# Attention and octonion FFN on one core: stacked operand rows in another order, and masked maxima by one vector instruction per head

## The chip, the cores and the metric

The kernel runs on one NeuronCore of a Trainium2 chip. The metric is the device time of one launch in microseconds; 1092.06 us is the median of three runs before the change. In the text PE is TensorE (matmuls), DVE is VectorE, ACT is ScalarE, POOL is GpSimd, and SP is the engine whose queue issues most of the DMAs.

## What is computed

The input x has 2 sequences of 1024 tokens with 512 features, all in float32. Cut to what matters:

```python
xn = layernorm(x)

# attention: 32 heads of 16 dimensions
q, k, v = split(xn @ w_qkv.T + b_qkv)
scores = q @ k.T / sqrt(16) + alibi[head, key]      # 1024 x 1024 per head
scores = where(query >= key, scores, -1e9)          # causal
attn = softmax(scores)
s = (attn @ v) @ w_out.T + b_out

# FFN with ternary weights in octonion products, hidden width 1360
gate, up = oct_linear(xn, w_gate), oct_linear(xn, w_up)
g = silu(oct_linear(silu(gate) * up, w_down))

return x + s * g
```

The softmax subtracts each query's maximum over its allowed keys. The change is in how these maxima are formed and in how the operands of the score products reach SBUF.

## The kernel before

**Stages.** A lead-in normalises the first tokens and projects the first heads; attention runs from some 37 us to some 800 us; the FFN follows and ends the span.

**Attention.** Heads go in groups of four (g, 8 per sequence), queries in halves of 512 (qc). One *unit* is (sequence, group, half), 32 in all. For each unit the kernel does two passes over the scores. The first forms each query's maximum: queries on the 128 partitions, keys along the columns (line 553, into one of three PSUM banks x0, x1, x2). For the first half of the queries only the diagonal part exists; for the second half every query also sees the 512 keys of the left half, which need no mask (`left`, line 567, one reduction per head). The diagonal part (`diagonal`, line 569) goes by blocks of 128 queries, tl = 0 to 3, with (tl + 1) x 128 keys each; one bank holds four heads of 128 keys, two of 256, one of 384 or one of 512. There VectorE first adds a triangular mask to the last 128 columns of each head, in place in PSUM, and then reduces the whole bank to one maximum per head (`mx`).

`split_max` joins `mx` and `left` and splits the maxima into two float32r parts (`rm`), `place_max` (line 612) turns them on TensorE and ScalarE copies them to SBUF (`mr`), and POOL issues two DMAs that put them into the two last rows of the stacked queries. The second pass (line 669) multiplies with those rows, so that the scores come out with the maximum already subtracted, now with keys on the partitions; ScalarE takes the exponential (`p`), and line 707 multiplies with the values.

**Stacked operands.** To keep float32 accuracy with float32r products, q and k are split into a high and a low part. A stack (`q_stack`, `k_stack`, rings of 4 and 5) has 128 rows: 64 rows hold four pairings of 16 dimensions (k: high, low, high, low; q: high, high, low, low), then come rows for the alibi term and the maxima. The contraction runs over the rows. `qk_items` projects q and k for two groups at a time (16 matmuls of 512 columns), splits them into `st` (ScalarE and VectorE), and SP writes `st` to `sp` in DRAM. `fill_k` and `fill_q` (lines 514 and 527) read them back, one DMA for each of the four pairings: 16 partitions, four heads, 512 elements each, 128 KB. `fill_k` also loads two alibi rows. One stack half needs four such transfers; attention has 64 stack halves, so 256 transfers.

**Weights.** `load_wq` (line 143) loads the q and k weights of the next two groups into `wqr` with two DMAs of 512 KB on SP's queue, and `compact_wq` (line 151) has POOL copy them into `wq`. The load is emitted with the last product of the groups before.

**Order.** All instructions are emitted by a planner that runs on the host when the kernel is built (from line 1092). It keeps model times of TensorE, VectorE and ScalarE, of the PSUM banks and of the fills, and emits next what it thinks is ready first: maxima (`next_max`), exponentials (`next_exp`), products with values, projections and others. Each engine then executes in that order; a wait that the planner did not foresee holds up all that follows on that engine. Its prices of a fill are in `try_fill` (line 1135), those of the maxima in `next_max` (line 1159). SP's queue carries weights, staged writes, fills, the writes of attention's output and the output's loads, in order. The trace shows that SP has eight semaphores in turn for its transfers, so that a transfer is issued when the eighth before it has landed.

The mask is a [128, 512] tile of which only columns 384 to 511, the triangle, are loaded (line 1030); later, in the FFN, the same tile serves as a buffer.

Of the kernel before, what the change touches and what calls it, by code (L numbers as in the profile page):

```python
# [10 lines left out]
F32 = mybir.dt.float32  # L11
F32R = mybir.dt.float32r
AF = mybir.ActivationFunctionType
ALU = mybir.AluOpType
AX = mybir.AxisListType
# [3 lines left out]
P = 128  # L19
B, S, D = 2, 1024, 512  # L20
NT = B * S
H, HD = 32, 16
NG = H // 4
KD = D // P
# [51 lines left out]
def kernel(  # L76
# [31 lines left out]
    NP = NG // 2  # L108
# [34 lines left out]
    def load_wq(gp, eng):  # L143
        t = wqp.tile([P, 2, KD, 2, 4, 32], F32, tag="wqr", name=f"wqr_{gp[0]}_{gp[1]}")
        for n in range(2):
            eng.dma_start(
                out=t[:, n].rearrange("p k w h e -> p (k w h e)"), in_=wqk[2 * gp[1] + n]
            )
        wq_raw[gp] = t
# [256 lines left out]

    def q_of(b, g, half):
        return q_ring[(2 * (b * NG + g) + half) % 4]  # L410

# [49 lines left out]
    def qk_items(b, gp):  # L461

        box = {}

        def product(which, c, kt):
            if (which, c, kt) == (0, 0, 0):
                if (b, gp) not in wq_tiles:
                    compact_wq((b, gp))
                parts[b, gp] = [
                    spill.tile([2, P, S], F32, tag=f"sp{w}", name=f"sp_{b}_{gp}_{w}")  # L470
                    for w in range(2)
                ]
            if kt == 0:
                box["ps"] = ps_m.tile([P, 512], F32, tag="m", name=f"pqk_{b}_{gp}_{which}_{c}")
            ps = box["ps"]
            pe(
                nc.tensor.matmul(  # L477
                    ps,
                    lhsT=wq_tiles[b, gp][:, kt, which, :],
                    rhs=xnT[:, kt, b * S + c * 512 : b * S + (c + 1) * 512],  # L480
                    start=(kt == 0),
                    stop=(kt == KD - 1),
                )
            )
            n = b * NP + gp + 1
            if (which, c, kt) == (1, 1, KD - 1) and n < B * NP:
                load_wq((n // NP, n % NP), sp_)
            if kt < KD - 1:
                return
            bias = bqk_sb[:, 1 + 2 * (which * NP + gp) :][:, 0:1]  # L490
            st = stg.tile([P, 2, 512], F32R, tag="st", name=f"st_{b}_{gp}_{which}_{c}")
            act_.activation(st[:, 0, :], ps, AF.Identity, bias=bias)
            dve_.scalar_tensor_tensor(
                st[:, 1, :], ps, bias, st[:, 0, :].bitcast(F32), ALU.add, ALU.subtract
            )
            sp_.dma_start(
                out=parts[b, gp][which][:, :, c * 512 : (c + 1) * 512].rearrange(
                    "l p n -> p l n"
                ),
                in_=st.bitcast(F32),  # L500
            )

        return [
            (858, lambda w=w, c=c, kt=kt: product(w, c, kt), "qk" if kt == KD - 1 else None)
            for w in range(2)
            for c in range(2)
            for kt in range(KD)
        ]
# [5 lines left out]
    def fill_k(b, g, half):  # L514

        k = k_of(b, g, half)
        for r in range(4):
            sp_.dma_start(
                out=k[r * HD : (r + 1) * HD].bitcast(F32),
                in_=heads(parts[b, g // 2][1], r % 2, g, half * 512, 512),  # L520
            )
        sp_.dma_start(
            out=k[64:66].bitcast(F32),
            in_=al_dram[:, 4 * g : 4 * g + 4, half * 512 : half * 512 + 512],
        )

    def fill_q(b, g, half):

        q = q_of(b, g, half)
        for r in range(4):  # L530
            sp_.dma_start(
                out=q[r * HD : (r + 1) * HD].bitcast(F32),
                in_=heads(parts[b, g // 2][0], r // 2, g, half * 512, 512),
            )

# [2 lines left out]
    def max_items(b, g, qc):  # L538

        tiles = {}  # L540

        def begin():
            for name in ("left", "mx")[1 - qc :]:
                tiles[name] = wk.tile([P, 4, 4], F32, tag=name, name=f"{name}_{b}_{g}_{qc}")

        def products(tl, first, count, c, n):
            x_banks[0] += 1
            ps = ps_x.tile(
                [P, 512], F32, tag=f"x{x_banks[0] % 3}", name=f"s1_{b}_{g}_{4 * qc + tl}_{c}_{first}"
            )  # L550
            for j in range(count):
                pe(
                    nc.tensor.matmul(  # L553
                        ps[:, j * n : (j + 1) * n],
                        lhsT=q_of(b, g, qc)[0 : NR - 2, first + j, tl * P : (tl + 1) * P],
                        rhs=k_of(b, g, c)[0 : NR - 2, first + j, :n],
                        start=True,
                        stop=True,
                    )
                )  # L560
            return ps[:, 0 : count * n].rearrange("p (h n) -> p h n", n=n)

        def left(tl, i):
            if (tl, i) == (0, 0):
                begin()
            ps = products(tl, i, 1, 0, 512)
            dve_.tensor_reduce(tiles["left"][:, tl, i : i + 1], ps, AX.X, ALU.max)

        def diagonal(tl, first, count):
            if (qc, tl, first) == (0, 0, 0):  # L570
                begin()
            n = (tl + 1) * P
            ps = products(tl, first, count, qc, n)
            block = ps[:, :, tl * P : n]
            dve_.tensor_tensor(
                block,
                block,
                mask[:, 384:512].rearrange("p (h n) -> p h n", h=1).to_broadcast([P, count, P]),
                ALU.add,
            )  # L580
            dve_.tensor_reduce(
                tiles["mx"][:, tl, first : first + count], ps, AX.X, ALU.max
            )

        items = []
        for tl in range(4):
            if qc:
                for i in range(4):
                    items.append((1, 512, False, lambda tl=tl, i=i: left(tl, i)))
            count = (4, 2, 1, 1)[tl]  # L590
            for i in range(0, 4, count):
                items.append(
                    (
                        count,
                        (tl + 1) * P,
                        True,
                        lambda tl=tl, i=i, count=count: diagonal(tl, i, count),
                    )
                )
        return items, tiles  # L600
# [251 lines left out]
    for b in range(B):  # L852
        for hh in range(2):
            n = 2 * b + hh
# [172 lines left out]
        busy(2)  # L1027
    compact_wq((0, 0))
    load_wv(0)
    sp_.dma_start(out=mask[:, 384:512], in_=cmask[:, 384:512])  # L1030
    sp_.dma_start(out=bv_sb, in_=bv.partition_broadcast(P))
    stat(4)
# [102 lines left out]
    def try_fill():  # L1135

        n, part = divmod(fills[0], 4)
        if n >= B * NG or len(qk_done) <= (n // 2 + 1 if n > 1 else part // 2):
            return
        if n == 0 and now[0] < qk_done[part // 2] - 4000:  # L1140
            return
        if unit_of(exps, E[0]) < 2 * (n - 2) + (0, 1, 2, 2)[part]:
            return
        (fill_q if part % 2 else fill_k)(n // NG, n % NG, part // 2)
        fills[0] += 1
        link[0] = max(now[0], link[0], qk_done[n // 2 + 1 if n > 1 else part // 2]) + (4500 if n else 3000)
        fill_at.append(link[0] + 2500)

    def try_fetch():
        for n, k in enumerate(fetches):  # L1150
# [8 lines left out]
    def next_max(pos):  # L1159
        if M[0] == len(maxs):  # L1160
            return []
        u, n, count, heads_in, cost, diagonal, emit = maxs[M[0]]
        fill = 4 * (u // 2) + 1 + 2 * units[u][2]
        if fills[0] <= fill or n == 0 and u >= 2 and u - 2 not in placed:
            return []

        def go():
            emit()
            M[0] += 1
            run_pe("R", ready, heads_in * max(cost * 0.417 + 18, 108))  # L1170
            end = run_dve(
                now[0] + START,
                heads_in * cost * 1.04 + 70 + (heads_in * 135 + 70) * diagonal,
            )
            take(x_free)[0] = end + END
            if n == count - 1:
                split_max(*units[u], mtiles[u])
                turns.append((u, run_dve(end, 500) + END))

        mpos = at[u] + (at[u + 1] - at[u]) * n / count  # L1180
        lead = size[1] + size[0] * 0.6
        ready = max(fill_at[fill], min(x_free))
        return [(ready, 4 if mpos < pos + lead else 5.5, 0, go)]
# [433 lines left out]
```

## Time and profile before

| | us |
|---|---|
| runs, without profile | 1090.71, 1092.06, 1093.07 |
| profiled execution, its own time | 1090.84 |
| its span (first to last instruction) | 1089.0 |
| PE, DVE, ACT, POOL busy | 1036.4, 678.9, 508.3, 173.8 |
| DMA moved | 104.04 MB, mean 96 GB/s |

By stage, from the windows view (busy us of each engine; the clock is the granted TensorE clock as a share of full speed):

| window, us | PE | DVE | ACT | clock | DMA busy | GB/s |
|---|---|---|---|---|---|---|
| 0 to 40 | 35.5 | 21.6 | 13.3 | 1.00 | 0.78 | 223 |
| 40 to 80 | 31.7 | 29.9 | 8.0 | 0.91 | 0.94 | 156 |
| 80 to 160 | 73.3 | 68.5 | 36.4 | 0.90 | 0.61 | 138 |
| 160 to 240 | 73.9 | 60.2 | 52.9 | 0.97 | 0.35 | 81 |
| 240 to 320 | 75.7 | 59.0 | 47.8 | 0.98 | 0.62 | 126 |
| 320 to 400 | 79.6 | 63.7 | 43.7 | 1.00 | 0.48 | 97 |
| 400 to 480 | 78.7 | 60.9 | 40.8 | 1.00 | 0.45 | 102 |
| 480 to 560 | 79.4 | 68.2 | 45.9 | 1.00 | 0.47 | 99 |
| 560 to 640 | 79.8 | 62.4 | 40.6 | 1.00 | 0.43 | 78 |
| 640 to 760 | 118.5 | 91.3 | 72.4 | 1.00 | | |
| 760 to 820 | 54.0 | 26.5 | 39.8 | 0.97 | 0.27 | 82 |

How to read these: a busy share is time in which the engine had an instruction under way. Matmuls overlap, and their ends are modelled, so a TensorE that is busy all the time need not run at its peak. "DMA busy" is the mean over the 16 DMA engines of the share of time in which their packets are under way; packets of one engine can overlap, so over a few microseconds it can exceed 1. In the groups by line nearly all vector, scalar and DMA instructions carry line 69, a helper that records them, so they are told apart by the tiles that they write and read: `s` are scores in PSUM, `mx` and `left` the maxima.

### The profile page before, as it was taken

What the parts mean: (1) busy time and instruction counts of PE and PEld (TensorE: products, weight loads), DVE (VectorE), ACT (ScalarE), POOL (GpSimd) and SP (SyncE); (2) the same over time, 40 slices, a digit from 0 to 9 for tenths busy, and PEclk for the clock granted to TensorE, in tenths of its full rate; (3) what the DMA queues carried; (4) which work ended last, traced back from release to release, by engine and by line L of the source; (5) the groups of instructions that cost most, each with busy time, mean ns of one, the idle gap of its engine ahead of it and who ended that gap; (6) DMA issues with size and microseconds to landing.
All of it is one profiled execution on the core that took longest, in us unless ns stands there. A gap on an engine that the chain in (4) does not pass through costs nothing.

```text
span 1089.0 us, 15459 instructions
## 1 busy us (share of the span) xinstructions
PE 1036.4 (95%) x5578; PEld 696.3 (64%) x5578; DVE 678.9 (62%) x1406; ACT 508.3 (47%) x958; POOL 173.8 (16%) x288
## 2 busy tenths in 40 slices
PE   8798988998999999999999999999999999999995
PEld 5554656674666667556667566665456678888784
DVE  6668888774988867878878778858342123141312
ACT  4032647654665544555645455665581213232322
POOL 7501014001010011010011000010011123332322
PEclk9999979999999999999999999999999999999998
DMA  6986563525374454355354337741141113030211
GB/s 226 175 157 161 137 124 108 89 52 116 82 154 89 123 85 81 99 136 95 74 128 65 82 78 116 137 89 50 35 132 49 49 59 116 1 116 1 79 38 39
DMA packets 73195, 104.04 MB, mean 96 GB/s; under 512 B 25896, under 2 KB 30640, under 8 KB 73120
## 3 DMA queue, kind: packets, MB, share of 16 engines
q1 hardware_dynamic: 69648, 98.28, 40.2%
q0 software_dynamic: 3424, 4.64, 1.7%
q8 instruction: 45, 0.74, 0.3%
q14 instruction: 30, 0.25, 0.1%
q10 hardware_dynamic: 48, 0.13, 0.0%
HBM read 69.39 MB, written 33.10 MB: 94 GB/s over the span
## 4 chain that ended last, share of the span: by engine, by line
PE 76%; DVE 8%; issue 5%; DMA 5%; ACT 4%; POOL 2%; SPq 0%; DVEq 0%; POOLq 0%; ACTq 0%
PE po L707 12%; PE s L669 12%; PE s L553 11%; PE pqk L477 9%; PE pu L1436 6%; PE pg L1436 6%; PE pd L1478 6%; PE pout L776 5%; PE pv L435 4%; DVE mx L69 3%; PE s L688 2%; DMA q_stack<-mr 1%; ACT p L69 1%; PE pm L618 1%; DVE s L69 1%
## 5 line engine op out<-in xcount | busy, mean ns | idle before, releaser
L69 ACT ACTIVATE p<-s 128x512 f32<-128x512 f32 x576 | 317.5, 596 | 205.0 <-PE s L688 114.0
L669 PE MATMUL s<-q_stack,k_stack 128*128 128x512 f32 (+3 forms) x768 | 252.5, 397 | 10.3 <-ACT p L69 5.1
L553 PE MATMUL s<-k_stack,q_stack 126*128 126x512 f32 (+3 forms) x768 | 235.5, 391 | 15.3 <-DVE mx L69 7.7
L69 DVE TENSOR_REDUCE mx<-s 128x1 f32<-128x384 f32 (+3 forms) x352 | 226.2, 643 | 11.6
L69 DVE TENSOR_REDUCE left<-s 128x1 f32<-128x512 f32 x256 | 163.8, 684 | 49.7 <-PE s L553 49.3
L669 PEld LDWEIGHTS s<-q_stack,k_stack 128*128 128x128 f32 x768 | 133.1, 190 | 82.7 <-ACT p L69 37.3
L553 PEld LDWEIGHTS s<-k_stack,q_stack 126*128 126x128 f32 x768 | 131.3, 192 | 67.5 <-issue 23.0
L707 PE MATMUL po<-p,v 128*32 128x512 f32 (+3 forms) x1536 | 142.2, 492 | 0.4 <-ACT p L69 0.4
L69 DVE TENSOR_TENSOR s<-s,mask 128x128 f32<-128x128 f32 (+2 forms) x352 | 123.9, 352 | 29.0 <-PE s L553 28.1
L477 PE MATMUL pqk<-xnT,wq 128*128 128x512 f32 x256 | 132.3, 618 | 8.1 <-POOL wq L69 6.9
L69 DVE SCALAR_TENSOR_TENSOR h<-pu,sc_u,sg 128x512 f32<-128x512 f32 (+1 forms) x44 | 33.0, 751 | 156.6 <-PE pu L1436 155.6
L69 POOL DMA_DIRECT2D q_stack<-mr x64 | 32.2, 508 | 615.5 <-ACT mr L69 615.5
L69 POOL TENSOR_TENSOR hs<-h,hs 128x512 fp32r<-128x512 f32 (+1 forms) x43 | 56.3, 1310 | 215.5 <-ACT hs L69 215.5
L688 PE MATMUL s<-mask_r,ident_r 128*128 128x256 f32 (+1 forms) x320 | 89.0, 278 | 0.0
L707 PEld LDWEIGHTS po<-p,v 128*32 128x32 f32 x1536 | 42.3, 109 | 72.5 <-issue 65.3
L69 ACT ACTIVATE sg<-pg,sc_g 128x512 f32<-128x512 f32 (+1 forms) x44 | 30.2, 687 | 100.2 <-PE pg L1436 100.0
L435 PE MATMUL pv<-wv,xnT 128*128 128x256 f32 x256 | 68.3, 392 | 0.1
L477 PEld LDWEIGHTS pqk<-xnT,wq 128*128 128x128 f32 x256 | 46.4, 195 | 33.8 <-issue 20.3
L69 ACT CAST hs<-h 128x512 fp32r<-128x512 f32 (+1 forms) x44 | 27.2, 619 | 85.3 <-DVE h L69 85.3
L776 PE MATMUL pout<-wo_sb,oT 128*128 128x512 f32 x128 | 62.7, 604 | 0.5 <-ACT oT L69 0.5
L688 PEld LDWEIGHTS s<-mask_r,ident_r 128*128 128x128 f32 x320 | 60.5, 189 | 2.7 <-issue 1.7
L435 PEld LDWEIGHTS pv<-wv,xnT 128*128 128x128 f32 x256 | 47.0, 193 | 17.1 <-issue 8.4
(144 smaller groups left out, 1074.8 us busy)
## 6 DMA issues: line engine op xcount, KB each, us to landing
sp<-st SPq DMA_DIRECT2D x32, 512.0 KB
k_stack<-sp SPq DMA_DIRECT2D x128, 128.0 KB
q_stack<-sp SPq DMA_DIRECT2D x128, 128.0 KB
wqr<-in_wqk_dram SPq DMA_DIRECT2D x16, 512.0 KB
xt<-in_x_dram SPq DMA_DIRECT2D x16, 256.0 KB
att<-o SPq DMA_DIRECT2D x32, 128.0 KB
ot<-att SPq DMA_DIRECT2D x16, 256.0 KB
proj<-y SPq DMA_DIRECT2D x16, 256.0 KB
```

The source lines that it names most:

```text
L69: ins = issue(*args, **kwargs)
L435: nc.tensor.matmul(ps[:, 0:256], lhsT=xnT[:, c, b * S + kt * P : b * S + (kt + 1) * P], rhs=wv_tiles[2 * b + hh][:, c, :], start=(c == 0), ...
L477: nc.tensor.matmul(ps, lhsT=wq_tiles[b, gp][:, kt, which, :], rhs=xnT[:, kt, b * S + c * 512 : b * S + (c + 1) * 512], start=(kt == 0), st ...
L553: nc.tensor.matmul(ps[:, j * n : (j + 1) * n], lhsT=q_of(b, g, qc)[0 : NR - 2, first + j, tl * P : (tl + 1) * P], rhs=k_of(b, g, c)[0 : NR ...
L618: nc.tensor.transpose(ps[0:8, tl * P : (tl + 1) * P], tiles["rm"][:, tl].rearrange("p l h -> p (l h)"), ident,)
L669: nc.tensor.matmul(ps[:, c0 : c0 + w], lhsT=k_of(b, g, kt // 4)[0:NR, h, kt % 4 * P : (kt % 4 + 1) * P], rhs=q[0:NR, h, 512 - w : 512], st ...
L688: pe(nc.tensor.matmul(out, lhsT=ident_r, rhs=rhs, start=False, stop=True))
L707: nc.tensor.matmul(po[32 * i : 32 * i + 32, 512 - w : 512], lhsT=v[:, kt, h * VC : h * VC + 32], rhs=p[:, i * part + c0 : i * part + c0 + ...
L776: nc.tensor.matmul(ps, lhsT=turned[t][:, c, :], rhs=wo_sb[0][:, c, :], start=(c == 0), stop=(c == KD - 1),)
L1436: nc.tensor.matmul(ps[:fs, :], lhsT=fw[mt][:, n0 + kt, 0:fs], rhs=part[:, kt, :], start=(kt == 0 and n == 0), stop=(kt == KD - 1 and n == 1),)
L1478: nc.tensor.matmul(pd, lhsT=hs[k][:fs, n, st * P : (st + 1) * P], rhs=fw[mt][:fs, 8:12, :].rearrange("p s n -> p (s n)"), start=(mt == 0 a ...
```

## The change

Five things change.

1. `fill_k` and `fill_q`: pairing r goes to the partitions r, r + 4, ..., r + 60 instead of r x 16 to r x 16 + 15. q and k are permuted alike, so the products sum the same terms. Source, bytes and number of DMAs stay.
2. `diagonal`: for each head one `tensor_tensor_reduce` adds a mask over all (tl + 1) x 128 columns, in place, and writes the maximum of the sum into `mx`. Before, there were one add and one reduction per bank.
3. The mask's columns 0 to 383 are set to zero by POOL, before its triangle is loaded, so that a mask of any of the four widths can be taken from the tile's end.
4. `load_wq` is emitted after the last staged write of `qk_items` instead of before it, so it stands behind that write on SP's queue.
5. The planner's prices: a fill occupies the link for 2600 ns instead of 4500 (3000 for the first group) and is ready 2200 ns later instead of 2500; a diagonal bank costs VectorE 100 ns per head on top of 1.04 ns a column, instead of 140 ns and 135 ns per head.

```diff
@@ qk_items, product
-            n = b * NP + gp + 1
-            if (which, c, kt) == (1, 1, KD - 1) and n < B * NP:
-                load_wq((n // NP, n % NP), sp_)
             if kt < KD - 1:
                 return
...
                 in_=st.bitcast(F32),
             )
+            n = b * NP + gp + 1
+            if (which, c, kt) == (1, 1, KD - 1) and n < B * NP:
+                load_wq((n // NP, n % NP), sp_)
@@ fill_k
-                out=k[r * HD : (r + 1) * HD].bitcast(F32),
+                out=k[r:64:4].bitcast(F32),
@@ fill_q
-                out=q[r * HD : (r + 1) * HD].bitcast(F32),
+                out=q[r:64:4].bitcast(F32),
@@ max_items, diagonal
             ps = products(tl, first, count, qc, n)
-            block = ps[:, :, tl * P : n]
-            dve_.tensor_tensor(
-                block,
-                block,
-                mask[:, 384:512].rearrange("p (h n) -> p h n", h=1).to_broadcast([P, count, P]),
-                ALU.add,
-            )
-            dve_.tensor_reduce(
-                tiles["mx"][:, tl, first : first + count], ps, AX.X, ALU.max
-            )
+
+            for j in range(count):
+                dve_.tensor_tensor_reduce(
+                    out=ps[:, j, :],
+                    in0=ps[:, j, :],
+                    in1=mask[:, 512 - n : 512],
+                    scale=1.0,
+                    scalar=-3.0e38,
+                    op0=ALU.add,
+                    op1=ALU.max,
+                    accum_out=tiles["mx"][:, tl, first + j : first + j + 1],
+                )
@@ lead-in
     load_wv(0)
+    pool_.memset(mask[:, 0:384], 0.0)
     sp_.dma_start(out=mask[:, 384:512], in_=cmask[:, 384:512])
@@ try_fill
-        link[0] = max(now[0], link[0], qk_done[n // 2 + 1 if n > 1 else part // 2]) + (4500 if n else 3000)
-        fill_at.append(link[0] + 2500)
+        link[0] = max(now[0], link[0], qk_done[n // 2 + 1 if n > 1 else part // 2]) + 2600
+        fill_at.append(link[0] + 2200)
@@ next_max
-                heads_in * cost * 1.04 + 70 + (heads_in * 135 + 70) * diagonal,
+                heads_in * cost * 1.04 + (heads_in * 100 if diagonal else 70),
```

## The prediction

> **What bounds the kernel now.** I read the page's busy shares and its chain of waits first, then the chain in order of time, the DMA queue's own instructions, the windows, and last the vector engine's groups by form.
>
> ```profile
> PE 1036.4 (95%) x5578; PEld 696.3 (64%) x5578; DVE 678.9 (62%) x1406; ACT 508.3 (47%) x958; POOL 173.8 (16%) x288
> PE 76%; DVE 8%; issue 5%; DMA 5%; ACT 4%; POOL 2%; SPq 0%; DVEq 0%; POOLq 0%; ACTq 0%
> 33.79 8.37 DMA sp<-st
> 45.59 7.22 DMA q_stack<-sp
> 62.50 7.97 DMA q_stack<-mr
> 721.75 7.06 DMA q_stack<-mr
> ```
>
> TensorE bounds it: 95% busy, 76% of the chain. What the change can win lies in the other quarter. The last four lines are the largest transfers on the chain (start, us, what): three follow each other before the first exponential at 70.6 us, the fourth comes at the end of attention.
>
> ```profile
> 38.00:40.00 2.00, 2.00 (x13) 1.73 (x13) 1.81 (x4) 0.00 (x0) 1.60 (x31) 1.00 1.02 413
> 46.00:48.00 2.00, 1.84 (x8) 1.04 (x6) 1.93 (x5) 0.00 (x0) 0.00 (x0) 1.00 1.07 131
> 40.00:80.00 40.00, 31.73 (x126) 20.12 (x128) 29.93 (x59) 8.02 (x12) 4.57 (x39) 0.91 0.94 156
> 480.00:560.00 80.00, 79.36 (x498) 50.47 (x497) 68.21 (x144) 45.86 (x84) 6.02 (x9) 1.00 0.47 99
> ```
>
> The windows end with granted clock, DMA share and GB/s. From 38 to 40 us weights and staged projections (128 partitions each) move at 413 GB/s; from 46 to 48 us only fills run, each into 16 neighbouring partitions, and with the DMA engines just as full (1.07) they make 131 GB/s. Fills are the slow transfers, and there are 256 of 128 KB.
>
> ```profile
> 32.28 1.29 SPq L69 DMA_DIRECT2D wqr<-in_wqk_dram  x2
> 33.79 0.38 SPq L69 DMA_DIRECT2D sp<-st  x1
> 42.18 1.73 SPq L69 DMA_DIRECT2D k_stack<-sp  x4
> ...
> 86.71 1.29 SPq L69 DMA_DIRECT2D wqr<-in_wqk_dram  x2
> 92.61 0.38 SPq L69 DMA_DIRECT2D sp<-st  x1
> ```
>
> SP's queue: the weight load (2 x 512 KB) stands ahead of the last staged write, and the fill at 42.18 waits for that write to land.
>
> ```profile
> L69 DVE TENSOR_REDUCE mx<-s 128x1 f32<-128x512 f32 x128 | 88.5, 691 | 4.3
> L69 DVE TENSOR_TENSOR s<-s,mask 128x128 f32<-128x128 f32 x256 | 74.6, 291 | 18.3 <-PE s L553 17.6
> L69 DVE TENSOR_TENSOR s<-s,mask 128x256 f32<-128x256 f32 x64 | 27.2, 425 | 7.9 <-PE s L553 7.7
> L69 DVE TENSOR_TENSOR s<-s,mask 128x512 f32<-128x512 f32 x32 | 22.1, 692 | 2.8 <-PE s L553 2.8
> ```
>
> An add costs 0.15 us and 1.06 ns a column (291, 425 and 692 ns), a reduction of 512 as much as an add of 512.
>
> **The masked maxima.** Removed are 352 adds (74.6 + 27.2 + 22.1 = 123.9 us) and 352 reductions into mx (226.2 us in the page's group): 350 us, over 512 heads 0.68 us each. Added are 512 instructions, 128 of each width 128, 256, 384 and 512. The trace has none of this kind. Bounds: from below a plain add over the same columns, 0.291 + 0.425 + 0.558 (interpolated) + 0.692 = 1.97 us for four heads, 128 times = 252 us; from above the slowest two-input row, the tail's y<-ga_more,s_posb with 1501 ns for 512 columns, 2.93 ns a column, 128 x 1280 columns = 480 us. In between: an add and a separate read-out at 0.15 us (sc_g, one column) is 328 us. I take the add, because its row has the same operands (scores from PSUM, mask from SBUF): DVE loses 98 us of its 679.
>
> [...]
>
> What this is worth is read from the chain. By stage from 80 to 560 us it holds 28 us of DVE mx and 12 us of DVE s, 40 in all; a head of 512 stands there with 0.22 + 0.02 + 0.69 = 0.93 us. With 0.69 it is 26% shorter: 10.4 us. But TensorE works in those stretches too: from 362.9 to 367.0 us the matmuls that start fill 3.2 of 4.1 us at their own pitch (0.23 us for 512 columns), from 453.6 to 458.7 us 4.6 of 5.05. TensorE is late next there and lets through 22% and 9% of 40 us, 8.8 and 3.6. Between 560 and 640 us the chain holds no DVE at all, so there it is worth nothing. I take **8 us** (3.6 to 10.4).
>
> **Fills over 64 partitions.** Same bytes, same instructions, same operands in the product; only rows move. The bounds are 131 GB/s (no gain) and 413; the nearest row that writes 64 partitions is the load of w_g, which together with a staged write makes 243 GB/s at 0.97 from 22 to 24 us. I take 243: a group of four falls from 4.0 to some 2.2 us.
>
> [...]
>
> **The weight load behind the staged write.** At 33.79 us the write was ready earlier (its DVE instruction ends at 32.6), so the issue wins 1.1 us, and 1 MB at 413 GB/s (2.5 us) no longer stands ahead of it; faster fills ahead of it give 1 to 2 more: the landing at 42.16 comes some 5 us sooner. The load now lies between that write and the next fills, where SP's 3.4 us of issuing covers it. The fill that lands at 52.81 gains 3 more by the rate, and the row of maxima at 62.50 (8 KB, 7.97 us amid the fills, the tile's median is 2.3) some 4. That is 12 us on the chain, but the window 40 to 80 shows what TensorE can take back: 8.3 us idle and 9% of 40 us lost to the clock, 11.9. I take **9 us** (1 to 11.9).
>
> The same move costs once. At 86.71 us the load now stands behind the write at 92.61, which waits for DVE. TensorE stood 2.62 us until 93.20 for the weights that this load brings; POOL's compaction is queued behind the landing, and behind it on POOL the next rows of maxima. It would come 6 us later; a shorter DVE queue there (four heads and one block of 512, some 2 us) and other work in front of the product reduce it. I take **+2 us** (0 to 6). Elsewhere a load has a unit (some 20 us) until it is used, and 5.6 us of landing are covered; if a product follows at once, it costs up to 6 again.
>
> **End of attention.** At 718 to 722 us eight fills are issued and the maxima's row behind them takes 7.06 us. At 243 GB/s the fills (1 MB) take 4.3 us instead of 8: **3 us** (0 to 4.8, down to the median).
>
> **At nothing.** Zeroing 384 mask columns on POOL: by the 64x2048 MEMSET (1.80 us) 0.34 us, within POOL's 3.94 us idle before 16.30; were the mask's load to wait for it, SP's next work but one is at 19.47. The planner's new prices change the order on TensorE, VectorE and SP throughout; the page cannot price that, zero is taken, and it is why the range is wider than the sum.
>
> **Sum.** 1090.84 us is the profiled execution's own time (span 1089.0), 1.2 below the median. -9 - 8 - 3 + 2 = -18: 1072.8, at the median **1074**. With all ends: -27.1 to +1.4, 1065 to 1093.
>
> **The rivals.**
> 1. All of it comes through: DVE's price is the reduction's back-to-back pitch (two in 1.29 us, so 0.60 instead of 0.93, 35% of 40 = 14 us), the lead-in gives 11.9 and the end 4.8, no wait for weights: -31, **1061**. For it: DVE is 85% busy from 480 to 560 us. Against: TensorE's 99% there. Were all 40 us of DVE gone from the chain alone it would be 1052.
> 2. Hidden anyway: the work that filled the lead-in's waits comes later, TensorE is the bound behind every DVE stretch, and only the end gives: -3, **1089**. For it: 560 to 640 us. Against: TensorE's real idle time at 53 us (5.2 us on q_stack<-sp).
> 3. Slower: the new instruction runs at the far row's 2.93 ns a column. 0.94 us a head against 0.68 is 130 us more on VectorE. Its 40 us on the chain become 55, and from 80 to 160 and 480 to 560 us, where it is already busy 68 of 80 us, 15 us more leave it over the window, so as much again: +30, less the transfers' 10: **1112**. It decides from where the chain pays over 10 us, 25% over 40 us: a head above 0.85 us on average. Against: the row with the same operands.
>
> **How the numbers follow.** Forecast 0.64, rivals 0.13, 0.11, 0.12. Within 0.2% (2.2 us, about what a measurement of this kernel can tell from no change) lies half of rival 2. Slower: rival 3 and a hundredth or two of the forecast with a bad order. Faster 0.80, same 0.06, slower 0.14. The range: 1052 (rival 1's far bound) to 1093 (the forecast's upper end).
>
> **What would show it.** Fills alone in a 2 us window at 200 GB/s or more; the last staged write of the lead-in landing before 38 us and the first exponential before 63; VectorE busy near 580 us, a head of 512 at 0.69; the last maxima's row landing within 4.5 us. Wrong if a head of 512 takes over 1.1 us, if the fills stay near 131 GB/s, or if new stretches of POOL wq or DVE stand on the chain.

## The result and the profile after

| | before | after |
|---|---|---|
| median of 4 runs each, us | 1091.99 | 1104.36 |
| lowest to highest, us | 1090.71 to 1093.07 | 1101.69 to 1106.1 |
| profiled execution, its span, us | 1090.84, 1089.0 | 1103.2, 1101.4 |

The ratio after to before is 1.0112, with a 95% interval of 1.0086 to 1.0137. The changed kernel is 12 us slower, where 18 us faster was forecast.

The profile after, in the order in which the prediction read that of before. First the page's busy row:

```profile
PE 1036.7 (94%) x5578; PEld 695.9 (63%) x5578; DVE 609.0 (55%) x1726; ACT 506.1 (46%) x958; POOL 173.8 (16%) x289
```

VectorE lost 70 us of busy time (678.9 before), TensorE none, and the span grew. The end of attention came later: the last exponential starts at 812.4 us, at 800.0 before, although the first starts at 60.4 instead of 71.2. So the lead-in gave 11 us, and attention lost 23 between those two marks.

The same windows as before (the columns are busy time and count of PE, weight loads, DVE, ACT and POOL, then granted clock, DMA share and GB/s):

```profile
38.00:40.00 2.00, 1.72 (x8) 0.92 (x7) 1.92 (x10) 0.00 (x0) 1.66 (x27) 1.00 1.01 306
46.00:48.00 2.00, 0.00 (x0) 0.00 (x0) 0.50 (x2) 0.00 (x0) 0.00 (x0) 1.00 0.83 207
40.00:80.00 40.00, 35.51 (x168) 23.44 (x166) 31.02 (x82) 9.35 (x15) 4.79 (x43) 0.96 0.57 159
480.00:560.00 80.00, 71.74 (x434) 43.90 (x427) 52.06 (x163) 39.10 (x73) 4.98 (x15) 0.94 0.27 79
```

Between 46 and 48 us only fills run, as before, and they make 207 GB/s instead of 131, with the DMA engines less full (0.83 against 1.07). From 40 to 80 us TensorE did 35.5 us of work instead of 31.7. The last row is one of the places where time is lost: TensorE was busy for 79.4 of these 80 us before, now for 71.7, at a clock of 0.94.

VectorE's groups by form (busy us in all, mean ns of one, idle time before them):

```profile
L69 DVE CUSTOM_DVE_ANT_0 s<-s,mask 128x512 f32<-128x512 f32 x128 | 86.6, 714 | 30.8 <-PE s L554 30.5
L69 DVE DVE_READ_ACCUMULATOR2_ANT mx<- 128x1 f32 x512 | 72.5, 142 | 0.0
L69 DVE CUSTOM_DVE_ANT_0 s<-s,mask 128x384 f32<-128x384 f32 x128 | 69.3, 585 | 24.7 <-PE s L554 24.5
L69 DVE CUSTOM_DVE_ANT_0 s<-s,mask 128x256 f32<-128x256 f32 x128 | 54.5, 442 | 12.6 <-PE s L554 10.5
L69 DVE CUSTOM_DVE_ANT_0 s<-s,mask 128x128 f32<-128x128 f32 x128 | 38.1, 298 | 8.2 <-PE s L554 4.9
```

Each of the 512 heads has become two instructions, 512 of each kind in the rows above: one that adds, and one that reads the maximum out (142 ns). The first costs about what a plain add costs (298, 442 and 714 ns against 291, 425 and 692). VectorE waits for TensorE's scores ahead of these adds for 70 us in all (the sum of the last numbers of the four rows; 28 us ahead of the adds before), so it is early more often than before.

What TensorE waited for, before and after (total us, times, longest us). First before, then after:

```profile
PE s L553 <- DVE mx L69: 7.7, 18, 2.3
PE pqk L477 <- POOL wq L69: 6.9, 3, 3.2
```

```profile
PE pqk L478 <- POOL wq L69: 25.9, 4, 8.6
PE s L554 <- DVE mx L69: 7.4, 18, 1.3
```

The waits for the maxima stayed as they were. Those of the projections for their weights grew by 19 us, more than the 12 us of the result. Where they lie is in TensorE's timeline (start, us, instruction, idle time before it and who ended it):

```profile
96.97 2.08 PE L478 MATMUL pqk<-xnT,wq 128*128 128x512 f32 x2 [8.60 <-POOL wq L69]
...
314.97 2.07 PE L478 MATMUL pqk<-xnT,wq 128*128 128x512 f32 x2 [6.69 <-POOL wq L69]
...
483.78 1.02 PE L478 MATMUL pqk<-xnT,wq 128*128 128x512 f32 x2
...
485.10 1.08 PE L554 MATMUL s<-k_stack,q_stack 126*128 126x512 f32 x6
493.62 2.07 PE L478 MATMUL pqk<-xnT,wq 128*128 128x512 f32 x2 [7.44 <-POOL wq L69]
```

These three, 22.7 us, are each the first product of a new pair of groups; the fourth, 3.2 us, stands at about the same time in before. SP's queue says why (start, us of issuing and of waiting to issue):

```profile
33.99 1.04 SPq L69 DMA_DIRECT2D sp<-st  x2
35.13 2.07 SPq L69 DMA_DIRECT2D wqr<-in_wqk_dram  x2
39.43 2.45 SPq L69 DMA_DIRECT2D k_stack<-sp  x4
...
473.49 11.59 SPq L69 DMA_DIRECT2D att<-o  x2
486.34 0.36 SPq L69 DMA_DIRECT2D sp<-st  x1
486.79 1.29 SPq L69 DMA_DIRECT2D wqr<-in_wqk_dram  x2
```

At 473.49 two writes of attention's output hold the queue for 11.6 us, 10.9 of them in waits for VectorE. The last staged write then waits 1.2 us more until VectorE has split the old pair's last product, which ended at 484.80; it is issued at 486.34, and only behind it the weights, at 486.79. They land and are copied by POOL, and the product starts at 493.62. At all three places it is the same: the load is issued 2.0 us after the end of the old pair's last product (at 90.12, 308.36 and 486.79), and the new pair's first product starts 6.6 to 6.9 us after that. So at these places a first product has to wait if it could follow the last one within 8.6 to 8.9 us (an estimate from these three, 2.0 + 6.6 to 6.9). The first rows show the same move in the lead-in, where it was meant to help: the write goes out ahead of the weights.

After the third of these waits more is lost than the wait. Windows of after, the column behind the five engines being the granted clock:

```profile
492.00:494.00 2.00, 0.38 (x1) 0.39 (x2) 0.00 (x0) 0.00 (x0) 1.29 (x7) 0.50 1.09 249
498.00:500.00 2.00, 2.00 (x6) 1.20 (x5) 0.69 (x1) 0.43 (x1) 0.00 (x0) 0.57 0.00 0
500.00:502.00 2.00, 2.00 (x16) 1.19 (x17) 1.78 (x6) 1.74 (x4) 0.00 (x0) 1.00 0.00 0
```

From 492 to 500 us the clock is 0.50 to 0.57. The two matmuls at 493.62 take 2.07 us, where the same form took 1.02 at 483.78. TensorE gets through 6 matmuls in the 2 us from 498, against 16 in those from 500 (some of these are the shorter products with the values).

### The profile page after: what moved, and what is told of

It reads as the page before. It is cut to its first block, busy times and chain, and to the rows that moved or that the text cites. A ratio compares the mean times of both kernels' runs of the same rounds, so it can differ in the third digit from the quotient of the medians.

```text
span 1101.4 us, 15618 instructions
## 1 busy us (share of the span) xinstructions
PE 1036.7 (94%) x5578; PEld 695.9 (63%) x5578; DVE 609.0 (55%) x1726; ACT 506.1 (46%) x958; POOL 173.8 (16%) x289
## 5 line engine op out<-in xcount | busy, mean ns | idle before, releaser
L69 DVE CUSTOM_DVE_ANT_0 s<-s,mask 128x384 f32<-128x384 f32 (+3 forms) x512 | 245.5, 510 | 76.4 <-PE s L554 70.4
L672 PE MATMUL s<-q_stack,k_stack 128*128 128x512 f32 (+3 forms) x768 | 258.8, 406 | 5.4 <-ACT p L69 5.1
L554 PE MATMUL s<-k_stack,q_stack 126*128 126x512 f32 (+3 forms) x768 | 228.3, 385 | 11.8 <-DVE mx L69 7.4
L478 PE MATMUL pqk<-xnT,wq 128*128 128x512 f32 x256 | 134.4, 622 | 27.1 <-POOL wq L69 25.9
L69 DVE DVE_READ_ACCUMULATOR2_ANT mx<- 128x1 f32 x512 | 72.5, 142 | 0.0
```

Of the source, the lines that this page charges most:

```text
L69: ins = issue(*args, **kwargs)
L478: nc.tensor.matmul(ps, lhsT=wq_tiles[b, gp][:, kt, which, :], rhs=xnT[:, kt, b * S + c * 512 : b * S + (c + 1) * 512], start=(kt == 0), st ...
L554: nc.tensor.matmul(ps[:, j * n : (j + 1) * n], lhsT=q_of(b, g, qc)[0 : NR - 2, first + j, tl * P : (tl + 1) * P], rhs=k_of(b, g, c)[0 : NR ...
L672: nc.tensor.matmul(ps[:, c0 : c0 + w], lhsT=k_of(b, g, kt // 4)[0:NR, h, kt % 4 * P : (kt % 4 + 1) * P], rhs=q[0:NR, h, 512 - w : 512], st ...
```

## The experiments

All are timed against the kernel before on the same chip. "Load early" means the weight load ahead of the pair's last staged write (before's place), "load late" behind it (after's place). Parts are numbered as in the change: 1 rows, 2 and 3 masked maxima with their mask, 4 weight load, 5 prices.

### What the load's place and the prices do

**e1_load_early**: after, with part 4 undone.

```diff
             if kt < KD - 1:
                 return
...
-            n = b * NP + gp + 1
-            if (which, c, kt) == (1, 1, KD - 1) and n < B * NP:
-                load_wq((n // NP, n % NP), sp_)
```

(The same three lines stand ahead of `if kt < KD - 1` again.)

> The kernel after, with the weight load back in front of the last staged write. Theory A (the load behind the staged write costs): in the trace after, TensorE stands 8.6, 6.7 and 7.4 us at three first projections whose weights were loaded late, and the units around two of them lose some 13 us each; with the load early these waits shrink to at most 3 us and the time falls by 20 to 35 us, to 1070 to 1084, below the kernel before. Rival B (the planner's new prices give a worse order of the engines' work, whatever the load does): at most 5 us are won, 1099 or more.

Measured: 1090.68 us, ratio 0.9995 (0.9972 to 1.0018). By the ratios the place of the load costs 12.8 us (1.0112 - 0.9995 = 0.0117 of 1092), and that is about as much as after is slower than before (12.2). TensorE's waits for weights fall from 25.9 to 12.0 us:

```profile
PE pqk L478 <- POOL wq L69: 12.0, 3, 5.6
```

The three of after were to shrink to at most 3 us; 3.2, none and 5.6 us are left of them. The result lies between the two expectations: with the load back in its place, the other four parts together win nothing, so something else takes back their gain.

Part of it shows at the same place of the order. SP's queue of e1:

```profile
462.15 0.38 SPq L69 DMA_DIRECT2D sp<-st  x1
462.78 11.56 SPq L69 DMA_DIRECT2D att<-o  x2
474.43 0.94 SPq L69 DMA_DIRECT2D wqr<-in_wqk_dram  x2
475.60 0.38 SPq L69 DMA_DIRECT2D sp<-st  x1
```

Even the early load now stands behind the writes, which wait 10.9 us for VectorE, and TensorE waits for it, 5.57 us at 481.0. The kernel before has one such write there, and it doesn't wait:

```profile
464.86 0.38 SPq L69 DMA_DIRECT2D sp<-st  x1
465.48 0.38 SPq L69 DMA_DIRECT2D att<-o  x1
465.95 1.30 SPq L69 DMA_DIRECT2D wqr<-in_wqk_dram  x2
```

That order comes from the planner, so from part 5.

**e2_load_late_only**: before with part 4 alone (the diff of the change, nothing else).

> The kernel before with the load behind the staged write and nothing else. Theory A: two of its seven later pairs of groups start within 3 us of the last staged write of the pair before (at 93 and at 477 us), so two waits of about 6 us more, each with a stretch of lower clock after it, less some 5 us in the lead-in: 1095 to 1110. Rival B: within 3 us of before, or faster by the lead-in's gain.

Measured: 1104.83 us, ratio 1.0129 (1.0093 to 1.0166), as theory A has it. TensorE's timeline of e2:

```profile
83.86 1.40 PE L553 MATMUL s<-k_stack,q_stack 126*128 126x256 f32 x4
96.67 2.08 PE L477 MATMUL pqk<-xnT,wq 128*128 128x512 f32 x2 [11.40 <-POOL wq L69]
```

The waits for weights are 23.1 us here (3 times), against 6.9 in before: 11.4 us instead of 2.6 at the third pair of groups, 8.6 instead of 1.1 at the seventh, and 3.2 at a place where before has them too. The part does this by itself, without the other instructions or the new order.

**e3_late_first_only**: after, with the load late in the lead-in (n == 1) and early elsewhere.

```diff
+            if (which, c, kt) == (1, 1, KD - 1) and 1 < n < B * NP:
+                load_wq((n // NP, n % NP), sp_)
             if kt < KD - 1:
...
-            if (which, c, kt) == (1, 1, KD - 1) and n < B * NP:
+            if (which, c, kt) == (1, 1, KD - 1) and n == 1:
```

> The kernel after, with the load behind the staged write for the first pair of groups alone, in the lead-in, and in front of it for the six others. Theory A: as the run with all loads early, and 1 to 5 us faster still, because the lead-in's last staged write lands sooner: 1068 to 1082. If the move of the load is worth nothing in the lead-in, the two runs agree within 1 us. Rival B: 1099 or more.

Measured: 1087.55 us, ratio 0.9957 (0.9937 to 0.9976), 3.1 us less than e1, just clear of the noise. Late in the lead-in helps, late elsewhere harms; both were expected. The total misses theory A's by 5.5 us, nearly as much as e1 misses its own. After differs from this run only by the six later loads, and by the ratios these cost 16.9 us (1.0112 - 0.9957 = 0.0155 of 1092).

**e4_prices_only**: before with part 5 alone.

```diff
-        link[0] = max(...) + (4500 if n else 3000)
-        fill_at.append(link[0] + 2500)
+        link[0] = max(...) + 2600
+        fill_at.append(link[0] + 2200)
...
-                heads_in * cost * 1.04 + 70 + (heads_in * 135 + 70) * diagonal,
+                heads_in * cost * 1.04 + (heads_in * 100 if diagonal else 70),
```

> The kernel before with the planner's new prices and nothing else, so the engines' work comes in the order of the kernel after, with the old fills, the old maxima and the early load. Rival B: slower than before by 10 us or more, 1102 or more. Theory A: the order by itself costs little, between 1085 and 1098.

Measured: 1138.62 us, ratio 1.0428 (1.0397 to 1.046). The waits view of e4:

```profile
PE s L553 <- DVE mx L69: 24.3, 55, 1.6
```

24.3 us in 55 waits for the maxima, 7.7 in 18 before. The prices can cost a lot; but here the maxima are still the old, slower ones and the fills too, so the prices are wrong for this kernel. What they do with the new instructions has to be tried there.

### The instructions without the new order

**e5_instructions_only**: after with parts 4 and 5 undone, so parts 1 to 3 alone.

> Parts 1 to 3 without the move of the load and without the planner's new prices: the order of before, with fast fills and the new maxima. With the load early the kernel after takes 1090.7, as before. Theory C (the new order gives back what parts 1 to 3 win, above all because it puts a write of attention's output, which waits for VectorE, in front of a weight load on SP): faster than before by 8 to 20 us, 1071 to 1083. Rival D (TensorE is the bound and hides what parts 1 to 3 win, whatever the order): within 5 us of before, 1086 to 1093.

Measured: 1073.93 us, ratio 0.9842 (0.9783 to 0.9901): 17 us faster. So in their sum the instructions do bring what was forecast of them. Against e1, which differs from it by part 5 alone, the new prices take back 16.7 us by the ratios (0.9995 - 0.9842 = 0.0153 of 1092).

**e6_spread_only** (part 1 in before) and **e7_ttr_only** (parts 2 and 3 in before).

> Fills over 64 partitions alone, all else as before. Theory C: the lead-in and the end of attention win 5 to 12 us, 1079 to 1086. Rival D: 1088 to 1092, because what the lead-in wins is taken back by the work that filled its waits. In both the DMA engines' share falls from 1.07 to some 0.8 in the windows of fills alone, as in the kernel after.

> The new maxima alone, with the old order, fills and load. VectorE's busy time falls from 679 to some 609 us as in the kernel after. Theory C: 3 to 10 us faster, 1081 to 1088. Rival D: within 3 us of before.

Measured: 1085.66 us, ratio 0.9949 (0.9924 to 0.9974), and 1085.94 us, ratio 0.9951 (0.9923 to 0.998). Each brings 5 to 6 us by itself, both within theory C. In e6 the rate of the fills is that of after, 206 GB/s from 48 to 52 us, but the DMA engines' share there is 0.65 to 0.74, lower than the 0.8 that was expected. What e6 wins shows in the lead-in alone: the first exponential starts at 66.6 us instead of 71.2, and from there to the last one it takes 730.0 us, 728.8 in before. In e7 the first starts where it did (71.1), and the stretch to the last takes 720.4 us. (The profiles are of single executions, 1.7 us above the median in e6 and 3.4 below it in e7.) Their sum, 0.0100, is less than e5's 0.0158; the intervals allow equality as well as some extra gain from having both.

**e8_load_mid**: after, with the load two staged writes earlier than the last one, but in the lead-in still behind the last.

```diff
-            if (which, c, kt) == (1, 1, KD - 1) and n < B * NP:
+            if (which, c, kt) == (int(n < 2), 1, KD - 1) and n < B * NP:
```

> The kernel after with each weight load but the lead-in's emitted two staged writes earlier (behind the product of the second of four, where the raw tile is long free), the lead-in's left where the kernel after has it. Theory A: the three waits of TensorE for late weights (8.6, 6.7 and 7.4 us) vanish, and the 5.6 us that the early load leaves at 475 to 481 us too: 1071 to 1082, below before. If the waits vanish and the time does not fall below 1086, what the waits cost was given back elsewhere and the bound is TensorE's own work.

Measured: 1075.9 us, ratio 0.9865 (0.9815 to 0.9914). One changed condition takes 27 us from after (1.0112 - 0.9865 of 1092). The waits view of e8:

```profile
PE pqk L478 <- POOL wq L69: 4.4, 2, 3.2
```

4.4 us instead of 25.9. The difference in spans, 28.6 us, is more than these 21.5; the mean granted clock rose as well, from 0.978 to 0.991.

### Order and place of the load together

**e9_old_order_load_mid**: e8 with the old prices (parts 1 to 3, load mid).

> Parts 1 to 3 with the order of before and the weight loads two staged writes earlier (the lead-in's last). If late weights are what is left to win: the 5.0 and 1.1 us that TensorE still waits for weights at 90 and 467 us in the run with the instructions alone go, and the time is 1065 to 1072. Otherwise as that run, 1073 to 1076.

Measured: 1064.91 us (1063.25 to 1066.17), ratio 0.9742 (0.9718 to 0.9767). It is the best of all and beats both kernels: 28 us faster than before. Of the two waits that were to go, the one of 5.0 us fell to 1.0 and the one of 1.1 us stayed. The first exponential starts at 61.7 us, in e5 at 67.2, so the late load in the lead-in has its part in the gain.

Where it does better than e8 is spread out. The windows with the largest difference, e8 and then e9:

```profile
240.00:320.00 80.00, 75.54 (x431) 46.01 (x424) 50.84 (x157) 46.54 (x82) 6.89 (x22) 0.98 0.32 97
```

```profile
240.00:320.00 80.00, 80.00 (x515) 51.34 (x508) 60.80 (x187) 53.85 (x96) 6.25 (x16) 1.00 0.45 131
```

With the old prices TensorE does not stop in this stage and starts 84 more matmuls. But 3.2 of the 4.5 us for which it stands in e8 are a wait for weights at 244 us that e9 has too, at 230 us, ahead of this window; so the window shows more than the order is worth. The page's chain of e9 (shares of the span) runs through TensorE for the most part:

```profile
PE 84%; issue 4%; ACT 4%; DVE 3%; POOL 2%; DMA 1%; SPq 0%; DVEq 0%; POOLq 0%; ACTq 0%
```

VectorE's share there is 8% in before and in e8.

**e10_max_price** and **e11_fill_price**: parts 1 to 3 with the load early, and one of the two new prices each (the lines of `next_max`, or those of `try_fill`).

> Parts 1 to 3 with the early load and of the new prices that of the maxima alone. The price is close to what the maxima take in the trace after (0.65 us pitch for 512 columns against 0.63). If this price makes the order in which the early load costs 17 us: 1085 to 1092. If the price of the fills does: 1070 to 1078.

> Parts 1 to 3 with the early load and of the new prices that of the fills alone. If this price makes the order that costs: 1085 to 1092. If that of the maxima does: 1070 to 1078. If only both together do, this run and the one with the maxima's price are both below 1080.

Measured: 1073.19 us, ratio 0.982 (0.9796 to 0.9844), and 1070.38 us, ratio 0.9792 (0.9771 to 0.9813). Neither price does harm alone; both together do (e1). So it isn't one wrong number but the order that comes of the pair.

**e12_old_order_load_late**: after with the old prices (parts 1 to 4).

> The kernel after with the planner's old prices: parts 1 to 4. Theory A: the load behind the staged write costs in the old order too, two waits for weights (near 88 and 468 us) of 6 us or more each, as in the run with the late load alone (14 us): 1083 to 1092, against 1073.9 with the early load. If the late load harms only together with the new order: 1071 to 1077.

Measured: 1082.11 us, ratio 0.9902 (0.9877 to 0.9926). Waits for weights are 21.2 us in 3, the longest 9.5, against 9.3 in 3 in e5. Both waits that were named are there, 9.5 and 8.5 us, and the lead-in wins: the first exponential starts at 61.5 us, in e5 at 67.2. The late load harms in the old order too, a little less than was expected.

All six combinations, with parts 1 to 3 in each (ratio to the kernel before on the same chip; in brackets its difference from 1 times 1092 us):

| load | old prices | new prices |
|---|---|---|
| early | e5 0.9842 (-17.3) | e1 0.9995 (-0.5) |
| late | e12 0.9902 (-10.7) | after 1.0112 (+12.2) |
| mid, late in the lead-in | e9 0.9742 (-28.2) | e8 0.9865 (-14.7) |

After is then the sum -17.3 (parts 1 to 3), +6.6 (part 4 in the old order) and +22.9 (part 5, given the late load), or, in the other order, -17.3, +16.7 (part 5, load early) and +12.8 (part 4, new prices). The 6.6 is the weakest of these: the intervals of e5 and e12 together are some 7 us either way, so it is read with their waits, 9.3 and 21.2 us. The others are clear of the noise.

## Why the prediction was wrong

**What bounds the kernel** was read rightly: TensorE is as busy in after as in before (1036.7 and 1036.4 us), and what moves the time is how long it stands, 25.9 us for weights against 6.9, and at what clock it runs after that, 0.50 behind the three long waits.

**Masked maxima and fills were right in their sum, but not term by term.** Their terms were -8 for the maxima, -3 for the end of attention, and of the lead-in's 12 those 7 that come from the rate (3 for the fill, 4 for the row of maxima): -18, if nothing of the 7 is taken back. Parts 1 to 3 alone (e5) measured -17.3, with an interval of -24 to -11. But the fills alone (e6) measured -5.6 (-8.3 to -2.8) against these 10, and in its profile nothing of it comes after the first exponential, so the 3 us at the end of attention do not show. The maxima alone (e7) measured -5.4 (-8.4 to -2.2) against 8. That the sum fits so closely is in part luck.
- The adding instruction: 86.6 + 69.3 + 54.5 + 38.1 = 248.5 us against the 252 that were taken from the plain add. But the forecast of one instruction per head failed: the read-out brings another 72.5 us. VectorE's busy time fell by 70 us. That is less than the 98 that were taken, and more than the 22 (350 - 328) that an add and a separate read-out would have left, because some 41 of these 72.5 us (an estimate: by durations alone 350 - 248.5 - 72.5 = 29 us would be saved, and 70 were) lie beside the next head's instruction or the end of the read-out's own. The timeline of after:

```profile
464.30 0.73 DVE L69 CUSTOM_DVE_ANT_0 s<-s,mask 128x512 f32<-128x512 f32 x1
464.95 0.14 DVE L69 DVE_READ_ACCUMULATOR2_ANT mx<- 128x1 f32 x1
```

  The read-out of the head before starts at 464.30 as well, together with this head's instruction, and this one's ends at 465.09: a head of 512 costs some 0.65 us from one to the next when no scores are waited for, near the 0.69 that was taken.
- Fills alone make 207 GB/s; 200 or more was to show the step right.
- The row of maxima, issue to landing: median 1.7 us (2.3 before); the slowest near the end of attention, at 708 us, take 4.4 to 4.7, about the 4.5 that was given for the last, and the later ones 1.7 to 2.4.

**The lead-in was right in its kind.** The first exponential starts at 60.4 us (before 63 was forecast). The last staged write landed later than forecast: the fill that waits for it is issued at 39.43, so it came some 2.7 us sooner than before (42.16), not 5, and was not there at 38. What the move of the load is worth there shows in e3: 3.1 us, inside the "1 to 5" of its expectation.

**The step that failed is the weight load's cost, "+2 us (0 to 6)", with its reason "Elsewhere a load has a unit (some 20 us) until it is used".** It was read at one place of the trace and carried to the others. The same trace shows that it isn't so. In before the new pair's first product starts 3.5 us after the end of the old pair's last one at 93.20 (the third pair), 13.1 us at 313.66 (the fifth) and 2.4 us at 477.43 (the seventh), and none of these loads had 20 us until it was used: they were issued 6.5, 17.3 and 11.5 us ahead. TensorE's timeline at the seventh:

```profile
474.51 0.80 PE L669 MATMUL s<-q_stack,k_stack 128*128 128x256 f32 x2
475.15 0.28 PE L688 MATMUL s<-mask_r,ident_r 128*128 128x256 f32 x1
...
477.43 1.12 PE L477 MATMUL pqk<-xnT,wq 128*128 128x512 f32 x2 [1.08 <-POOL wq L69]
```

The load for it was issued at 465.95, and POOL delivered it 1.08 us too late as it was. The staged write, behind which it now stands, was issued at 476.62. What the late load adds to the waits there (us, early and late load, from TensorE's timelines):

| first product of | old order, before and e2 | old order, e5 and e12 | new order, e1 and after |
|---|---|---|---|
| the third pair | 2.6, 11.4 | 5.0, 9.5 | 3.2, 8.6 |
| the fifth pair | 0, 0 | 0, 0 | 0, 6.7 |
| the seventh pair | 1.1, 8.6 | 1.1, 8.5 | 5.6, 7.4 |

So there are two such places in the old order and three in the new one, and at the one place that was read the wait grew by 8.8, 4.5 and 5.4 us, where +2 (0 to 6) was taken. At the seventh pair most of the 7.4 us in after stands with the early load too: there it is the two output writes ahead, which the new order brings. In time all six later loads cost 16.9 us (after against e3). Together with the gain in the lead-in, the move measures +14.1 us in before's kernel (e2), +6.6 with the other instructions in the old order (e12 against e5) and +12.8 in the new one (after against e1). The half sentence "if a product follows at once, it costs up to 6 again" named the mechanism; the places that meet its condition weren't counted, and it stands in no sum.

**The second failed step is the planner's order "at nothing".** It costs 16.7 us with the load early, 13.4 with it mid and 22.9 late. That the profile can't price an order was true; that zero is the middle of what it can do was not shown by anything. The prediction named "new stretches of POOL wq or DVE" on the chain as what would make it wrong. The chain on the page of after covers the last 4% of the span alone and shows neither. The waits show the first. For the second there is the chain of e1: parts 1 to 3 in the old order bring VectorE's share down from 8% in before to 3% in e5, and with the new prices it is 7% again.

**The rivals.** Rival 3 (slower) came out on the right side by luck, with the wrong mechanism: a head takes 0.51 us on the average of the four widths, 0.65 with its read-out, under the 0.85 from which it decided. Rival 2, everything hidden, is refuted by e5; rival 1's 1061 is what e9 comes near, 1064.9, with little of what rival 1 excluded, waits for weights (5.2 us), but e9 is another kernel than the one it was about.

**Left open.** Why both prices together make a worse order when neither does alone isn't settled. In e8, where waits for weights are down to 4.4 us, the new order still loses 13.4 us to e9. Waits for the maxima are one part (7.0 us in 16 in e8, 3.1 in 5 in e9); on the page's chain VectorE holds 8% in e8 and 3% in e9, 7% in e1 and 3% in e5. Which choice of the planner brings this, no run here shows.

## What to carry to other kernels

When a transfer is moved behind another on a queue that issues in order, as SP's did here (two waiting writes held the weight load back for 11.6 us), list every place where it is issued, and for each the time from the old issue to the first use and what the new predecessor waits for; one place read is not the rule for all. Where a schedule is planned from prices, truer prices are a change of their own with either sign: measure the new instructions in the old order first, then the order. And where a part helps in one stage and harms in the others, it can be had in that stage alone, as e9 has it.

## What the hardware showed unexpectedly

Spreading the rows made the transfer faster (131 to 207 GB/s where only fills run) and its issue slower. The fills' instructions on SP's queue, before and then after (ns, minimum, median and maximum):

```profile
L69 SPq DMA_DIRECT2D k_stack<-sp x128: 302/424/1802, 27.3 to 719.5; - x128
```

```profile
L69 SPq DMA_DIRECT2D k_stack<-sp x128: 532/593/1587, 28.4 to 736.4; - x128
```

With 16 rows four apart instead of 16 neighbours an issue takes 0.59 us in the median instead of 0.42, with the same bytes and the same count. Four fills of 128 KB, 0.52 MB, then take 4 x 0.59 = 2.4 us to issue, which is 220 GB/s (an estimate from the median): so near the 207 that were measured that the issuing queue is the likely next limit of the fills (no run here tried it). For this speaks that the rate is the same in e6, 206 GB/s, where the DMA engines' share is only 0.65 and 0.74 in the two windows from 48 to 52 us.

The read-out of a maximum takes 142 ns, of which more than half is hidden, by the estimate of 41 of 72.5 us above. And after the three waits of 8.6, 6.7 and 7.4 us in after the granted clock stays at 0.50 for some 3.4, 3.9 and 6.1 us of work more (estimates from windows of 2 us), so these waits cost more than the waits view says.
